# A 3x3 convolution taken by row pairs: four products of row sums and tap sums in place of six

## The chip, the core and the metric

The kernel runs on one core of a Trainium2 chip. The metric is device time in microseconds (us), from the start to the end of one execution. The kernel before takes 14228.68 us (median of 3 runs, 14222.29 to 14232.47).

The engines of the core work beside each other, each through its own instructions in order: PE (matrix products into PSUM), DVE and POOL (elementwise work on SBUF; DVE also reads PSUM), ACT (functions of one input, with a table of functions that has to be loaded), SP (starts transfers). They wait for each other through semaphores.

## The reference, cut to what matters

Four layers run over 16 images of 192 channels and 32 x 32 pixels. Only layer 0 is touched. Of layer 0 the change touches one operation, the last:

```
seq = group_norm(x) as tokens                       # 1024 tokens of 192 channels
y   = seq + vil_block(seq)                          # layer norm, up-projection to 384, causal
                                                    # convolution over 4 tokens, q, k, v, gates,
                                                    # mLSTM over 12 heads, down-projection
y   = y + silu(seq @ w_lin + b_lin)
out = conv2d(y, conv2_w, 3 x 3, padding 1) + conv2_b    # 192 -> 192 channels
batch_norm(out)                                     # statistics over all 16 images
```

All data is float32. The batch norm needs the convolution of all images, so layers 1 to 3 start when the last image's convolution is done.

## The kernel before, in words

`layer0` handles one image at a time. Image 0 stands alone; a loop (L751) runs images 1 to 15; in iteration b the convolution of image b-1 is worked in between the steps of image b; the convolution of image 15 stands alone behind the loop (L755). The loop ends each iteration with a barrier of all engines.

**An image** (`image`, L403) has three stages.
- The head: group norm (L88 to L107, with two tiny products L91 and L99), channel norm (products with `on192` and, on the squares `sq`, again; L122, L124, L128, L129, L131), the up-projection `w_up` (24 products of 512 columns, all at L39), the causal convolution on DVE (L435, L439), the gates (L455, L466, scans L480, L484), the projections `w_q` and `w_k` (L39), and `qs` (products L549, DVE L553).
- The chunk phase, written out by hand under `tc.manual_schedule()`: twelve times `scores` (products L613 into four PSUM tiles, ACT L620, DVE L624, POOL L627 with `mask`), with `turned` (L584, L594), `leave` (L683, L686, POOL L687) and `finish` (L639, L646, L658, ACT L650, DVE L651, product L671, ACT L672 and L673, DVE L674) as soon as a chunk of 128 tokens has what it needs.
- The tail: `w_lin` and `w_down` (products L731), ACT L735 (Silu), DVE L736, and DVE L739, which writes the sum into the padded image `ypad`.

Outside the chunk phase a scheduler orders the instructions of each engine; inside it, the order is as written, and the scheduler may put tail products between.

**The convolution** (`conv3`, L365) is a generator. `fill(n)` (L563) takes n steps from it. `ypad` holds channels 0 to 127 in one half (e = 0) and channels 128 to 191 in the other, there twice on 64 partitions each, one copy moved by one column by two transfers (`both`, L744), so that two of the three columns go in one product. The result comes in three groups (m): channels 0 to 127 for the upper and the lower 16 rows, and channels 128 to 191 for both halves, side by side on PSUM's partitions. Each group is 15 steps; a step is one product of 512 columns, or two side by side for the third group. So an image takes 45 steps. A group adds up in the one PSUM tile `pc`; then ACT writes it out (L394), DVE takes statistics (L395), SP stores it (L397). The steps are spread: `fill(15)` ahead of the chunk phase (L567), which the scheduler spreads over the head; `fill(2)` in each `finish` (L669) and in each of the rounds without one (L704); 1 (L705) and 8 (L708) at the end.

PSUM tiles for all other products rotate over six (`ps`, L164); the four for `scores` are among them. Layers 1 to 3 (`LayersB`) are planned by another part of the kernel, which the change does not touch.

Of the kernel before, what the change touches and what calls it, by code (L numbers as in the profile page):

```python
# [11 lines left out]
F32 = mybir.dt.float32  # L12
BF16 = mybir.dt.bfloat16
AF = mybir.ActivationFunctionType
ALU = mybir.AluOpType
# [16 lines left out]
def half(hf):  # L32
    return slice(hf * HL, (hf + 1) * HL)
# [113 lines left out]
def rows(ap):  # L147

    return ap.rearrange("p (h w) -> p h w", w=W)
# [3 lines left out]
def layer0(tc, cx, NB, ydram, sdram, w1d):  # L153
    nc, I = cx.nc, cx.I
    with ExitStack() as ctx:
        wp = ctx.enter_context(tc.tile_pool(name="a_w", bufs=1))
# [3 lines left out]
        psc = ctx.enter_context(tc.tile_pool(name="a_psc", bufs=1, space=PSUM))  # L160
# [24 lines left out]
        prp = pre.enter_context(tc.tile_pool(name="a_pre", bufs=1))  # L185
# [14 lines left out]

        hmask = wp.tile([128, 4 * HW1], F32, name="hmask")
        nc.sync.dma_start(hmask, I["c_hmask"])
        b_if = []
        for nm, eng in (("b_i", nc.sync), ("b_f", nc.scalar)):
            t = wp.tile([128, 1], F32, name="v_" + nm)
# [9 lines left out]
        nc.scalar.dma_start(conv_k, I["conv_k"].rearrange("(k p) t -> p k t", p=128))  # L217
        mask = wp.tile([128, 2 * CH], F32, name="mask")

        blocks = wp.tile([128, 4, DH], F32, name="blocks")  # L220
        nc.vector.tensor_copy(blocks, hmask.rearrange("p (j d) -> p j d", d=HW1)[:, :, 0:DH])
        blk = blocks.rearrange("p j d -> p (j d)")

# [78 lines left out]
        p = ps()  # L302
# [30 lines left out]
        w_c2 = wp.tile([128, 9, C], F32, name="w_c2")  # L333
        nc.sync.dma_start(w_c2, I["conv2_wT"][0:128])
        w_c2p = wp.tile([128, 2, 3, C], F32, name="w_c2p")
        for u in range(2):
            r = slice(64 * u, 64 * u + 64)
            taps = I["conv2_wT"][128:C].rearrange("p (y x) o -> p y x o", x=3)
            nc.sync.dma_start(w_c2p[r, 0], taps[:, :, u, :])
            nc.sync.dma_start(w_c2p[r, 1], taps[:, :, 2, :])  # L340
# [8 lines left out]
        b_down, b_lin, c2_b = vec3("b_down"), vec3("b_lin"), vec3("conv2_b")  # L349
        x_in = wp.tile([128, 3, L + 3], F32, name="x_in")  # L350
        nc.gpsimd.memset(x_in, 0.0)
        ypad = wp.tile([128, 2, H + 2, W + 2], F32, name="ypad")
        nc.gpsimd.memset(ypad, 0.0)
        vas = []
        for i in range(2):
            t = wp.tile([128, NH, DH], F32, name="va%d" % i)
# [7 lines left out]

        def conv3(b):  # L365

            st = sm.tile([128, 3, 6], F32, tag="st", name="st")
# [3 lines left out]
            def window(r, e, y, x, hf):  # L371
                return ypad[r, e, 16 * hf + y : 16 * hf + y + 16, x : x + W]

            for m in range(3):
                p = psc.tile([128, HL], F32, name="pc")

                parts = [(m, slice(0, 128), slice(0, 128))] if m < 2 else [
                    (0, slice(128, C), lower), (1, slice(128, C), upper)
                ]
                for n in range(15):  # L380
                    for hf, o, r in parts:
                        y, x = divmod(n, 3) if n < 9 else ((n - 9) % 3, 2 * (n >= 12))
                        if n < 9:
                            w_, v = w_c2[:, n, o], window(slice(0, 128), 0, y, x, hf)
                        elif n < 12:
                            w_, v = w_c2p[:, 0, y, o], window(slice(0, 128), 1, y, x, hf)
                        elif hf == 0:
                            w_, v = w_c2p[lower, 1, y, o], window(lower, 1, y, x, hf)
                        else:
                            w_, v = w_c2p[upper, 1, y, o], window(upper, 1, y, x - 1, hf)  # L390
                        nc.tensor.matmul(p[r, :], lhsT=w_, rhs=v, start=(n == 0), stop=(n == 14))  # L391
                    yield
                yo = wk2.tile([128, HL], F32, tag="yo", name="yo", bufs=1)
                nc.scalar.activation(yo, p, AF.Identity, bias=c2_b[:, m // 2 : m // 2 + 1])  # L394
                nc.vector.bn_stats(st[:, m, :], yo)  # L395
                for hf, o, r in parts:
                    nc.sync.dma_start(here(o)[:, half(hf)], yo[r, :])  # L397
            stats = lambda o: sdram[bass.ds(b, 1), o].rearrange("o p s -> p (o s)")
            nc.scalar.dma_start(stats(slice(0, 128)), st[:, 0:2, :].rearrange("p h s -> p (h s)"))
            for hf, r in enumerate((lower, upper)):  # L400
                nc.scalar.dma_start(stats(slice(128, C))[:, 6 * hf : 6 * hf + 6], st[r, 2, :])

        def image(b, conv):  # L403
            xn = big.tile([P6, 2, L], F32, name="xn")
# [6 lines left out]
            sq = big.tile([P6, 2, L], F32, tag="kT", name="sq")  # L411
# [32 lines left out]


            cx.ln_exp()
            it = gp.tile([128, L], F32, name="it")
            lf = gp.tile([128, L], F32, name="lf")
            e1 = gp.tile([128, L], F32, name="e1")

            p = ps()
            for g in range(3):
                for q in range(4):
# [7 lines left out]
            raw = gp.tile([128, HL], F32, name="raw")  # L461
            nc.scalar.copy(raw, p)
            for j in range(2):
                for hf in range(2):
# [13 lines left out]
            for c in range(NCH):  # L478
# [4 lines left out]
            at = gp.tile([128, L], F32, name="at")  # L483
# [20 lines left out]
            kT = big.tile([128, 3, L], F32, tag="kT", name="kT")  # L504
# [19 lines left out]
            nc.vector.tensor_copy(dec.rearrange("p g c -> p (g c)"), p[:, 0 : 3 * NCH])  # L524


            itg = big.tile([128, 3, L], F32, name="itg")
# [35 lines left out]
            def fill(n):  # L563
                for _ in range(n):
                    next(conv, None)

            fill(15)  # L567


            cst = big.tile([128, 3, DH], F32, name="cst")  # L570
# [119 lines left out]
            with tc.manual_schedule():  # L690
                ready = begun = 0
                for n in range(3 * NCH // 2):
                    scores(n)
                    if begun < NCH and 2 * n + 1 >= 3 * begun:
                        turned(begun)
                        begun += 1
                    if normed:
                        leave()

                    if 2 * n >= 3 * ready + 3:  # L700
                        finish(ready)
                        ready += 1
                    else:
                        fill(2)  # L704
                fill(1)  # L705
                leave()
                finish(ready)
                fill(8)  # L708
                leave()
# [12 lines left out]
            for n in range(3):  # L722
                e = n // 2
                parts = [(n, slice(0, 128), slice(0, 128))] if n < 2 else [
                    (0, slice(128, C), lower), (1, slice(128, C), upper)
                ]
                pl, pd = ps(), ps()
                for p, w_, v, k in ((pl, w_lin, xn, 2), (pd, w_down, hT, 3)):
                    for i in range(k):
                        for hf, o, r in parts:  # L730
                            nc.tensor.matmul(  # L731
                                p[r, :], lhsT=w_[:, i, o], rhs=v[:, i, half(hf)], start=(i == 0), stop=(i == k - 1)
                            )
                lin = wk2.tile([128, HL], F32, tag="lin", name="lin")
                nc.scalar.activation(lin, pl, AF.Silu, bias=b_lin[:, e : e + 1])  # L735
                nc.vector.tensor_add(lin, lin, xr[:, n, :])  # L736
                for hf, o, r in parts:
                    x = 0 if r == upper else 1
                    nc.vector.scalar_tensor_tensor(  # L739
                        ypad[r, e, 1 + 16 * hf : 17 + 16 * hf, x : x + W], rows(pd[r, :]),  # L740
                        b_down[r, e : e + 1], rows(lin[r, :]), op0=ALU.add, op1=ALU.add,
                    )

        def both():  # L744

            lower, upper = slice(0, 64), slice(64, 128)
            nc.sync.dma_start(ypad[upper, 1, 1:17, 0:W], ypad[lower, 1, 1:17, 1 : 1 + W])
            nc.sync.dma_start(ypad[lower, 1, 17:33, 1 : 1 + W], ypad[upper, 1, 17:33, 0:W])

        image(0, iter(()))  # L750
        with tc.For_i(1, NB, 1) as b:  # L751
# [107 lines left out]
class LayersB:  # L859
# [1314 lines left out]
```

## Time and profile before

| what | value |
|---|---|
| median of the runs | 14228.68 us |
| the profiled execution | 14239.71 us |
| its span, first to last instruction | 14237.9 us |
| image 0 and what is ahead of it | 0 to 206.7 us |
| loop, 15 iterations | 206.7 to 3049.5 us |
| spacing of iterations | by turns 188.1 and 190.9 us, save the first: mean 189.5 |
| last convolution alone | 3049.8 to 3094.4 us |
| layers 1 to 3 | the rest, about 11140 us |

How to read the views: the page lists each engine's busy time and, in 40 slices of the span (356 us each), its share in tenths. The window view gives, for a stretch, each engine's busy time and instruction count, and the clock that PE was granted as a share of full speed. The timeline lists instructions in order with start, duration, engine, line, tile written and read, how many were merged, and in brackets the idle time ahead and what ended it. A float32 product shows as two records; with 512 columns two records take 0.86 us.

### The profile page before, as it was taken

What the parts mean: (1) busy time and instruction counts of PE and PEld (TensorE: products, weight loads), DVE (VectorE), ACT (ScalarE), POOL (GpSimd) and SP (SyncE); (2) the same over time, 40 slices, a digit from 0 to 9 for tenths busy, and PEclk for the clock granted to TensorE, in tenths of its full rate; (3) what the DMA queues carried; (4) which work ended last, traced back from release to release, by engine and by line L of the source; (5) the groups of instructions that cost most, each with busy time, mean ns of one, the idle gap of its engine ahead of it and who ended that gap; (6) DMA issues with size and microseconds to landing.
All of it is one profiled execution on the core that took longest, in us unless ns stands there. A gap on an engine that the chain in (4) does not pass through costs nothing. (4 is left out here: it accounts for less than half of the span.)

```text
span 14237.9 us, 185312 instructions
## 1 busy us (share of the span) xinstructions
PE 12109.3 (85%) x68762; PEld 4953.3 (35%) x68762; DVE 11818.6 (83%) x9084; ACT 8686.4 (61%) x12225; POOL 10919.5 (77%) x6319
## 2 busy tenths in 40 slices
PE   8999999987888888888888888888888888888877
PEld 4444444442232333333333333333333333333323
DVE  4444444446899999999999999999999999999996
ACT  3333333335666676767676767667676767676665
POOL 2222222215789999999999999999999999999995
PEclk9999999998999999999999999999999999999988
DMA  1000000013344544444444445454544444444432
GB/s 29 15 16 15 16 16 14 14 39 125 129 161 136 164 142 159 153 166 158 146 160 145 161 142 164 153 165 141 166 137 165 141 162 163 156 155 151 147 123 90
DMA packets 702526, 1707.93 MB, mean 120 GB/s; under 512 B 125456, under 2 KB 260064, under 8 KB 693984
## 3 DMA queue, kind: packets, MB, share of 16 engines
q1 hardware_dynamic: 688928, 1693.28, 36.0%
q8 instruction: 555, 9.09, 0.3%
q10 hardware_dynamic: 12736, 3.04, 0.1%
q14 instruction: 307, 2.51, 0.1%
HBM read 1338.12 MB, written 341.15 MB: 118 GB/s over the span
## 5 line engine op out<-in xcount | busy, mean ns | idle before, releaser
L1995 POOL TENSOR_TENSOR xs<-du,bb 128x1024 f32<-128x1024 f32 x3072 | 7191.9, 2365 | 313.2 <-DVE h L2003 309.0
L2003 DVE TENSOR_TENSOR_SCAN h<-h,xs 128x1024 f32<-128x1024 f32 x2688 | 6149.3, 2288 | 280.9 <-ACT h L1988 191.4
L1988 ACT ACTIVATE h<-dl,A 128x1024 f32<-128x1024 f32 x3072 | 3415.4, 1113 | 2517.6 <-DVE hc L2012 2358.9
L2012 DVE TENSOR_TENSOR hc<-h,cb 128x1024 f32<-128x1024 f32 x2688 | 3290.2, 1224 | 267.4 <-DVE h L2003 7.3
L2045 PE MATMUL acc<-hc,sel 128*32 128x256 f32 x24576 | 2046.3, 419 | 916.0 <-DVE hc L2012 691.3
L815 PE MATMUL mm<-pad,dg 128*128 128x512 f32 (+1 forms) x5580 | 2672.0, 616 | 97.2 <-ACT pad L815 37.5
L627 POOL TENSOR_TENSOR D<-D,mask 128x256 f32<-128x256 f32 x768 | 543.4, 740 | 2102.2 <-DVE D L624 2102.2
L2045 PEld LDWEIGHTS acc<-hc,sel 128*32 128x32 f32 x24576 | 546.3, 113 | 2899.6 <-DVE hc L2012 1583.4
L815 PEld LDWEIGHTS mm<-pad,dg 128*128 128x128 f32 (+1 forms) x5580 | 958.0, 182 | 1476.4 <-issue 1293.1
L2008 POOL TENSOR_TENSOR hc<-hc,cb 128x1024 f32<-128x1024 f32 x384 | 905.3, 2357 | 149.8 <-DVE hc L2003 145.7
L815 PE MATMUL mm<-pa,wgt 128*128 128x512 f32 (+1 forms) x1408 | 795.9, 691 | 111.2 <-ACT p L815 52.4
L2003 DVE TENSOR_TENSOR_SCAN hc<-h,xs 128x1024 f32<-128x1024 f32 x384 | 875.5, 2280 | 13.7 <-ACT h L1988 9.4
L2053 PE MATMUL acc<-one,zero 128*128 128x512 f32 x1498 | 804.4, 667 | 0.0
L815 POOL TENSOR_TENSOR dlh<-dlh,e 128x512 f32<-128x512 f32 x384 | 490.6, 1278 | 233.8 <-ACT e L815 233.7
L815 POOL TENSOR_TENSOR c<-cx 96x768 f32<-96x768 f32 (+4 forms) x510 | 650.4, 1299 | 0.6 <-ACT cx L815 0.6
L815 PE MATMUL mm<-c,xT 128*96 128x256 f32 x2048 | 570.1, 420 | 64.5 <-ACT c L815 64.4
L815 POOL TENSOR_TENSOR duh<-dlh,xx 128x512 f32<-128x512 f32 x384 | 538.1, 1401 | 30.1
L391 PE MATMUL pc<-ypad,w_c 128*64 128x512 f32 (+1 forms) x1152 | 480.4, 664 | 74.2 <-PEq L751 41.5
L2032 PE MATMUL acc<-y,ident 128*128 128x512 f32 x576 | 350.6, 694 | 185.3 <-ACT y L2064 185.2
L624 DVE SCALAR_TENSOR_TENSOR D<-D,s 128x256 f32<-128x256 f32 x768 | 271.6, 415 | 255.4 <-ACT D L620 255.3
L2064 ACT COPY y<-acc 128x512 f32<-128x512 f32 x384 | 410.8, 1070 | 115.2 <-PE acc L2045 114.4
L815 PE MATMUL mm<-xd,dtw 108*128 108x512 f32 x768 | 455.7, 677 | 15.5 <-ACT p L815 13.7
(333 smaller groups left out, 15741.3 us busy)
## 6 DMA issues: line engine op xcount, KB each, us to landing
dl<-dld SPq DMA_DIRECT2D x768, 512.0 KB
du<-dud SPq DMA_DIRECT2D x768, 512.0 KB
bb<-xdr SPq DMA_DIRECT2D x256, 512.0 KB
cb<-xdr SPq DMA_DIRECT2D x256, 512.0 KB
dld<-dlh SPq DMA_DIRECT2D x384, 256.0 KB
dud<-duh SPq DMA_DIRECT2D x384, 256.0 KB
dg<-dqd SPq DMA_DIRECT2D x270, 192.0 KB
dg<-dvd SPq DMA_DIRECT2D x180, 144.0 KB
```

What stands on the lines that cost most here:

```text
L391: nc.tensor.matmul(p[r, :], lhsT=w_, rhs=v, start=(n == 0), stop=(n == 14))
L627: nc.gpsimd.tensor_mul(d, d, mask)
L815: return f(out, *args, **kw)
L1988: self.nc.scalar.activation(self.h[u % 2], self.dl[n % 2], AF.Exp, scale=self.A[:, blk, n : n + 1])
L1995: self.nc.gpsimd.tensor_mul(self.xs[u % 3], self.du[n % 2], self.bb[blk])
L2003: self.nc.vector.tensor_tensor_scan(o, h, x, 0.0, op0=ALU.mult, op1=ALU.add)
L2008: self.nc.gpsimd.tensor_mul(h, h, self.cb[u % BLOCKS])
L2012: self.nc.vector.tensor_mul(self.hc[u % 3], self.h[u % 2], self.cb[u % BLOCKS])
L2032: nc.tensor.matmul(acc, lhsT=self.cx.ident, rhs=self.y[:, g, half(pair)], start=True, stop=False)
L2045: nc.tensor.matmul(self.acc[rows4(q), q4(s)], lhsT=self.sel, rhs=part(q), start=False, stop=(s + blk == BLOCKS),)
L2053: self.nc.tensor.matmul(self.acc, lhsT=cx.zero.to_broadcast([128, 128]), rhs=cx.one.to_broadcast([128, HL]), start=False, stop=False,)
L2064: self.nc.scalar.copy(y.rearrange("p (s w h) -> p s h w" if k % 2 == 0 else "p (s h w) -> p s w h", s=2, **turn), self.acc.rearrange("p (s ...
```

## The change

The nine taps form three rows. For output rows 2j and 2j+1 the input rows 2j to 2j+3 are combined once into four sums (`four`): r0-r2, r1+r2, r2-r1, r1-r3; the weights once into four as well: g0, (g0+g1+g2)/2, (g0-g1+g2)/2, g2. Four products p0 to p3 then give the two output rows as p1+p2+p0 and p1-p2-p3. Products p1 and p2 use r1+r2 and r2-r1, p0 and p3 the other two. Each product is over 16 row pairs x 32 columns = 512 columns and takes five steps (three columns of channels 0 to 127, two of the rest). So channels 0 to 127 need 4 x 5 steps, and channels 128 to 191 2 x 5 double steps: 30 in place of 45. There are six groups in place of three, all in the one tile `pc`; p1 is written out by ACT (`one`), the others are added by DVE.

The sums are made by eight POOL operations in `both`, at the head of each iteration. `ypad` shares its memory with `kT` and is cleared by POOL once per image. The weights come in 15 transfers in place of 5, and ten DVE operations make the combined ones, once. To make room, some tiles share others' memory (`yo` with `it`, `one` with `fc`, `lin` with `lf` and `e1`, `sq` with `itg`, `raw` with `at`).

```diff
+        for y, i in ((0, 0), (1, 2), (2, 3)):
+            nc.sync.dma_start(w_c2[:, i], I["conv2_wT"][0:128, 3 * y : 3 * y + 3])
+            for u in range(2):
+                r = slice(64 * u, 64 * u + 64)
+                nc.sync.dma_start(w_c2p[r, i, 0], I["conv2_wT"][128:C, 3 * y + u])
+                nc.sync.dma_start(w_c2p[r, i, 1], I["conv2_wT"][128:C, 3 * y + 2])
+        for w in (w_c2, w_c2p):
+            w = w.rearrange("p i x o -> p i (x o)")
+            nc.vector.tensor_add(w[:, 1], w[:, 0], w[:, 3])
+            nc.vector.tensor_add(w[:, 1], w[:, 1], w[:, 2])
+            nc.vector.scalar_tensor_tensor(w[:, 2], w[:, 2], -2.0, w[:, 1], op0=ALU.mult, op1=ALU.add)
+            nc.vector.tensor_scalar(w[:, 1], w[:, 1], 0.5, None, op0=ALU.mult)
+            nc.vector.tensor_scalar(w[:, 2], w[:, 2], 0.5, None, op0=ALU.mult)
...
-        ypad = wp.tile([128, 2, H + 2, W + 2], F32, name="ypad")
-        nc.gpsimd.memset(ypad, 0.0)
+        kT = wp.tile([128, 3, L], F32, name="kT")
+        pad = kT.rearrange("p g t -> p (g t)")[:, 0 : 2 * (H + 2) * (W + 2)]
+        four = wp.tile([128, 2, 4, H // 2, W + 2], F32, name="four")
...
+            for e, o in enumerate((slice(0, 128), slice(128, C))):
+                yo = gp.tile([128, L], F32, tag="it", name="yo")[0:np_]
+                one = big.tile([128, L], F32, tag="fc", name="one")[0:np_, 0:HL]
+                for group in ((1,), (2,), (0,), (3,)) if e == 0 else ((1, 2), (0, 3)):
+                    p = psc.tile([128, HL], F32, name="pc")
+                    parts = [(i, p) for i in group] if e == 0 else [(group[0], p[lower]), (group[1], p[upper])]
+                    for n in range(5):
+                        for k, (i, q) in enumerate(parts):
+                            term(q, i, n, o, upper if k else lower)
+                        yield
+                    for i, q in parts:
+                        if i == 1:
+                            nc.scalar.activation(one, q, AF.Identity, bias=c2_b[0:np_, e : e + 1])
+                        elif i == 2:
+                            nc.vector.tensor_add(even, rows(one), rows(q))
+                            nc.vector.tensor_sub(odd, rows(one), rows(q))
+                        elif i == 0:
+                            nc.vector.tensor_add(even, even, rows(q))
+                        else:
+                            nc.vector.tensor_sub(odd, odd, rows(q))
+                    yield
+                for hf in range(2):
+                    nc.vector.bn_stats(st[0:np_, 2 * e + hf, :], yo[:, half(hf)])
+                nc.sync.dma_start(here(o), yo)
...
-            fill(15)
+            fill(12)
...
                     else:
-                        fill(2)
+                        fill(1)
+                nc.gpsimd.memset(pad, 0.0)
                 fill(1)
                 leave()
...
         def both():
...
+            for e in range(2):
+                r = [ypad[:, e, k : k + H - 1 : 2, :] for k in range(4)]
+                nc.gpsimd.tensor_sub(four[:, e, 0], r[0], r[2])
+                nc.gpsimd.tensor_add(four[:, e, 1], r[1], r[2])
+                nc.gpsimd.tensor_sub(four[:, e, 2], r[2], r[1])
+                nc.gpsimd.tensor_sub(four[:, e, 3], r[1], r[3])
```

A group now takes six calls of the generator: five steps and one that only writes out.

More of the change, by code (lines that the diff above doesn't have):

```diff
@@ L199, in layer0 @@
         mh_b = vec("mh_b", 128, nc.scalar)
-        hmask = wp.tile([128, 4 * HW1], F32, name="hmask")
+        hmask = prp.tile([128, 4 * HW1], F32, name="hmask")
         nc.sync.dma_start(hmask, I["c_hmask"])
@@ L218, in layer0 @@
         mask = wp.tile([128, 2 * CH], F32, name="mask")
-        blocks = wp.tile([128, 4, DH], F32, name="blocks")
+        blocks = prp.tile([128, 4, DH], F32, name="blocks")
         nc.vector.tensor_copy(blocks, hmask.rearrange("p (j d) -> p j d", d=HW1)[:, :, 0:DH])
@@ L332, in layer0 @@
             nc.sync.dma_start(t, I[nm].rearrange("(k p) o -> p k o", p=p))
[L333 to L340, printed above, removed]
+        w_c2 = wp.tile([128, 4, 3, C], F32, name="w_c2")
+        w_c2p = wp.tile([128, 4, 2, C], F32, name="w_c2p")
+        for y, i in ((0, 0), (1, 2), (2, 3)):
[11 more added lines that the diff above has]
+            nc.vector.tensor_scalar(w[:, 2], w[:, 2], 0.5, None, op0=ALU.mult)
         def vec3(name):
@@ L351, in layer0 @@
         nc.gpsimd.memset(x_in, 0.0)
-        ypad = wp.tile([128, 2, H + 2, W + 2], F32, name="ypad")
-        nc.gpsimd.memset(ypad, 0.0)
+        kT = wp.tile([128, 3, L], F32, name="kT")
+        pad = kT.rearrange("p g t -> p (g t)")[:, 0 : 2 * (H + 2) * (W + 2)]
+        ypad = pad.rearrange("p (e y x) -> p e y x", e=2, x=W + 2)
+        four = wp.tile([128, 2, 4, H // 2, W + 2], F32, name="four")
         vas = []
@@ L365, in conv3 @@
         def conv3(b):
-            st = sm.tile([128, 3, 6], F32, tag="st", name="st")
+            st = sm.tile([128, 4, 6], F32, tag="st", name="st")
             here = lambda o: ydram[bass.ds(b, 1), o].rearrange("o p l -> p (o l)")
             lower, upper = slice(0, 64), slice(64, 128)
[L371 to L388, printed above, removed]
-                        else:
-                            w_, v = w_c2p[upper, 1, y, o], window(upper, 1, y, x - 1, hf)
-                        nc.tensor.matmul(p[r, :], lhsT=w_, rhs=v, start=(n == 0), stop=(n == 14))
@@ new lines, in term @@
+            def term(out, i, n, o, r):
+                if n < 3:
+                    w_, v = w_c2[:, i, n, o], four[:, 0, i, :, n : n + W]
+                elif n == 3:
+                    w_, v = w_c2p[:, i, 0, o], four[:, 1, i, :, 0:W]
+                else:
+                    x = 2 if r == lower else 1
+                    w_, v = w_c2p[r, i, 1, o], four[r, 1, i, :, x : x + W]
+                nc.tensor.matmul(out, lhsT=w_, rhs=v, start=(n == 0), stop=(n == 4))
+            for e, o in enumerate((slice(0, 128), slice(128, C))):
+                np_ = o.stop - o.start
+                yo = gp.tile([128, L], F32, tag="it", name="yo")[0:np_]
+                even, odd = (yo.rearrange("p (j u w) -> p j u w", u=2, w=W)[:, :, u, :] for u in range(2))
+                one = big.tile([128, L], F32, tag="fc", name="one")[0:np_, 0:HL]
[14 more added lines that the diff above has]
+                            nc.vector.tensor_add(even, even, rows(q))
+                        else:
+                            nc.vector.tensor_sub(odd, odd, rows(q))
@@ L392, in conv3 @@
                     yield
[L393 to L397, printed above, removed]
+                for hf in range(2):
+                    nc.vector.bn_stats(st[0:np_, 2 * e + hf, :], yo[:, half(hf)])
+                nc.sync.dma_start(here(o), yo)
@@ L398, in conv3 @@
             stats = lambda o: sdram[bass.ds(b, 1), o].rearrange("o p s -> p (o s)")
             nc.scalar.dma_start(stats(slice(0, 128)), st[:, 0:2, :].rearrange("p h s -> p (h s)"))
-            for hf, r in enumerate((lower, upper)):
-                nc.scalar.dma_start(stats(slice(128, C))[:, 6 * hf : 6 * hf + 6], st[r, 2, :])
+            nc.scalar.dma_start(stats(slice(128, C)), st[lower, 2:4, :].rearrange("p h s -> p (h s)"))
         def image(b, conv):
@@ L410, in image @@
             h = big.tile([P6, 2, L], F32, tag="h", name="h")
-            sq = big.tile([P6, 2, L], F32, tag="kT", name="sq")
+            sq = big.tile([P6, 2, L], F32, tag="itg", name="sq")
             rstd = big.tile([P6, L], F32, tag="fc", name="rstd")
@@ L446, in image @@
             cx.ln_exp()
-            it = gp.tile([128, L], F32, name="it")
-            lf = gp.tile([128, L], F32, name="lf")
-            e1 = gp.tile([128, L], F32, name="e1")
+            it = gp.tile([128, L], F32, tag="it", name="it")
+            lf = gp.tile([128, L], F32, tag="lf", name="lf")
+            e1 = gp.tile([128, L], F32, tag="e1", name="e1")
             p = ps()
@@ L460, in image @@
                     )
-            raw = gp.tile([128, HL], F32, name="raw")
+            raw = gp.tile([128, L], F32, tag="at", name="raw")[:, 0:HL]
             nc.scalar.copy(raw, p)
@@ L482, in image @@
                 )
-            at = gp.tile([128, L], F32, name="at")
+            at = gp.tile([128, L], F32, tag="at", name="at")
             nc.vector.tensor_tensor_scan(at, lf, it, 0.0, op0=ALU.add, op1=ALU.max)
@@ L503, in image @@
             qT = big.tile([128, 3, L], F32, name="qT")
-            kT = big.tile([128, 3, L], F32, tag="kT", name="kT")
             for m in range(3):
@@ L524, in image @@
             nc.vector.tensor_copy(dec.rearrange("p g c -> p (g c)"), p[:, 0 : 3 * NCH])
-            itg = big.tile([128, 3, L], F32, name="itg")
+            itg = big.tile([128, 3, L], F32, tag="itg", name="itg")
             for g in range(3):
@@ L733, in image @@
                             )
-                lin = wk2.tile([128, HL], F32, tag="lin", name="lin")
+                lin = gp.tile([128, L], F32, tag="lf" if n == 1 else "e1", name="lin")[:, 0:HL]
                 nc.scalar.activation(lin, pl, AF.Silu, bias=b_lin[:, e : e + 1])
```

## The prediction

> **What bounds the kernel now.** I read the page's slices first, then the window view by stage, then the timeline of one iteration (968.0 to 1156.1 us). From the page:
>
> ```profile
> span 14237.9 us, 185312 instructions
> ...
> PE   8999999987888888888888888888888888888877
> ...
> DVE  4444444446899999999999999999999999999996
> ...
> POOL 2222222215789999999999999999999999999995
> ```
>
> Layer 0 is the first nine slices: PE has nine tenths, DVE four, POOL two. Later DVE and POOL are full, and nothing is changed there. So only PE's path through layer 0 counts. From the window view (PE, PEld, DVE, ACT, POOL, then PEclk):
>
> ```profile
> 968.00:976.00 8.00, 7.91 (x18) 3.56 (x19) 5.07 (x14) 2.82 (x3) 0.00 (x0) 0.81 0.23 38
> 1054.50:1064.00 9.50, 8.23 (x73) 4.98 (x77) 2.64 (x6) 2.75 (x7) 3.58 (x5) 0.64 0.08 29
> 1064.00:1140.00 76.00, 72.85 (x1070) 43.61 (x1062) 33.56 (x81) 30.78 (x82) 42.02 (x57) 1.00 0.05 16
> 57.00:81.00 24.00, 23.97 (x52) 10.28 (x56) 18.18 (x19) 5.92 (x9) 0.00 (x0) 0.87 0.00 0
> 124.00:195.00 71.00, 58.19 (x1043) 42.17 (x1035) 37.14 (x89) 39.38 (x94) 45.78 (x62) 1.00 0.05 13
> ```
>
> The last two rows are image 0, which has no convolution beside it: its chunk phase takes 71 us, that of the loop some 84. So 30 steps of 0.86 us (26 us of PE) lengthen that phase by 13 us; the other half hides in PE's waits. The clock column is the second finding: PE runs at 0.64 in the 9.5 us behind one wait. The timeline of PE shows which:
>
> ```profile
> 1050.20 1.99 PE L549 MATMUL ps<-isc,sel 32*128 32x512 f32 x12
> 1054.49 1.21 PE L613 MATMUL s<-at,itg 32*128 32x128 f32 x13 [2.30 <-DVE qs L553]
> ...
> 1057.46 0.85 PE L594 MATMUL ps<-ident,kT 128*128 128x128 f32 x3
> 1059.46 3.78 PE L391 MATMUL pc<-ypad,w_c 128*128 128x512 f32 x4 [1.16 <-ACT yo L394]
> 1063.17 0.73 PE L613 MATMUL s<-at,itg 32*128 32x128 f32 x16
> ```
>
> An idle time of 2.30 us, then four records take 3.78 us; at full clock they take 1.88 (next round). Steps of the convolution are work and also what keeps PE's clock up.
>
> **The change, part by part**, against that iteration.
>
> *Removed.* 15 of 45 steps: 12.9 us of PE per image. The order of the changed kernel's instructions shows where: the head keeps 5 of 15 steps, all ahead of the channel norm; 5 more stand between L549 and the first L613; the chunk phase and the tail hold 20 in place of 30.
>
> *Start of the iteration: slower, +2.6 us.* PE's first product now waits for the second POOL sum, its fourth for the sixth; L91, L99 and the channel norm stand behind them in PE's queue. The price of a sum over 544 elements is not in the trace. Nearest rows: POOL L627 over 256 takes 740 ns, `dlh` over 512 takes 1278, so 2.1 ns for each further element and 1.35 us; the strided L687 (915 for 384) and `duh` (1401 for 512) bound it at 1.2 to 1.5. So the first product goes at 970.8 and not at 968.1; at half clock step, L91, step, L99 end at 975.2; the third step follows, the sixth sum is there at 976.2, two more steps end at 978.3. There the channel norm's products start, which started at 975.7. Ends: +1.5 (clock up early) and +5.0 (DVE's small operations of the group norm each wait for a POOL operation). For the latter the rows disagree: DVE L667 takes 243 ns alone and up to 782 beside POOL, but L2012, also two inputs from SBUF, 1202 to 1227 beside a full POOL. I go with L2012, which has 2688 instances.
>
> The Trainium skill (SBUF — State Buffer, "Who interferes with whom") says that a DVE instruction with two SBUF inputs and a POOL instruction that reads SBUF shut each other out for a whole instruction. By it L95, L96 and L97 would wait some 3.4 us (an estimate), and the sum below would come to about +16 us instead; L667 agrees, L2012 does not.
>
> *Head without filler: +3.8 us.* The channel norm's second products (on `sq`) and the up-projection follow idle times that steps filled. Without these I get 2.4 us ahead of `sq` (975.7 plus 8 records end at 979.2, `sq` is ready at 981.6) and 3.3 us ahead of `w_up` (L128 0.68, L129 1.06, L131 1.2 and hand-overs). By the 2.30 us above both lower the clock. Image 0 shows the price: from the first `w_up` product to DVE's L435, 7.5 us (57.03 to 64.57) against 4.6 (989.32 to 993.92); from the first `sq` product to the second L128 5.4 against 4.1. I take +2.7 and +1.4, less 0.3 for the steps that stood ahead of `w_up`. From L435 on DVE sets the pace to the gates (16.1 us in both images). Ends: -0.3 (clock holds) and +5.6 (all eight `sq` records at half clock, 3.0 later, and 2.9). Between L455 and L466 one step goes: -0.2.
>
> The skill's TensorE: Matmul & The Clock Gate ("Why this matters for your kernels") puts the limit at gaps over about 3 us. By it the gap ahead of `sq` would be free, and the sum 21 us lower; the trace's 2.30 us with a clock of 0.64 behind it speaks against.
>
> *Start of the chunk phase: -3.2 us.* The five steps now fill the 2.30 us and PE stays at full clock: they end at 1056.5, the first L613 goes there (1054.5 before). DVE's L624 stands behind the two new additions of p2, which need the group's end: 1058.6 in place of 1056.5. The second round's L613 then goes at 1060.0 instead of 1063.2, since the wait for L394 (1.16) and the half clock are gone. POOL's masks come next: two rounds of 2.8 with a `vw` of 0.84 between, from 1059.1, let the first `finish` go on at 1065.6; with its two steps L671 starts at 1067.9, before at 1071.1. Ends -1 (masks back up further) and -5.
>
> *Rest of the chunk phase: -5.0 us.* Rounds without `finish`: from L683 to the next L613 0.87 us in image 0 (144.97 to 145.83), 2.6 with two steps (1082.85 to 1085.44), 3.8 where L394 is waited for (1102.22 to 1106.00). With one step, none and one: -0.9, -2.9, -0.9. In `finish` two steps cost only 0.4 (L658 to L671: 1.7 in image 0, 2.1 in the loop), since L651 is awaited anyway; one fewer there: -0.3. DVE's additions (0.7 each) and statistics (1.4) stand where DVE waits 1.9 us for L673. Ends -3 and -6.
>
> *Tail: +0.3 us.* The scheduler moves the first Silu and five `w_lin`/`w_down` products into the last rounds. The Silu costs table loads (1.28 each) ahead of L672 and L673, as in image 0; two of them are on the path. One step also waits for ACT and DVE to write p1 and p2 out. I get the last L683 3.9 us later, and behind it four DVE operations (2.8 us) ahead of L686; but 8.5 products are left where 14 were (-4.7). Ends -1.5 and +3.
>
> *Hidden.* The clearing by POOL (2.02 us, L353) stands ahead of two L687, in a gap from 1129.7 to 1133.8; without that, +2.0 per image. At the start ten transfers (0.65 each on SP) and ten DVE operations (5.2 us) fall in DVE's 7.8 us wait ahead of L131 in image 0; without that up to +5 once. The last convolution, alone: 30 steps, but six write-outs and the POOL sums ahead; 43.5 us against 44.7: -1, from -3 to +4.
>
> **Sum.** 2.6 + 3.8 - 0.2 - 3.2 - 5.0 + 0.3 = -1.7 us. Every second iteration takes 190.9 us rather than 188.1, with a clock of 0.61 in its first 8 us and 0.58 behind the 2.30 us wait; half of that should go: -0.6 on the mean. So -2.3 x 15 - 1 = -35.5 us: 14239.7 becomes 14204.2 on the profiled execution's scale, which is 11.0 above the median; on the median's 14193.
>
> **Rivals.**
> - *The head goes cold.* Place: from the iteration's start to `w_up`. PE starts late and in pieces, so the clock stays at half through the five steps (they end at 980.3, so +4.6), both norms and the first `w_up` products: `sq` +3.0, `w_up` +2.9, -0.3, sum +10.2; the other terms as above, -8.1: +2.1 for the iteration. It decides from a loss of 8.7 us in the head on (the 8.1 of the other terms and the 0.6 of every second iteration). 15 x 2.1 - 1 for the last convolution: +31, 14260. For it: the 0.81 and 0.61 with PE's start as it is. Against: image 0's `sq` phase got its clock back.
> - *The clock holds in the head.* Only the wait for POOL is left: 2.6 - 0.3 in place of 6.4, -6.4 per iteration, 14132. For it: between 976 and 990 the clock is 1.00. Against: that is with filler.
> - *What goes was free.* POOL's masks and the DVE additions hold the chunk phase, gaining 5 rather than 8.2 and losing what the head loses: within 15 us of zero, 14225.
> - *Fewer products in name only*: excluded; the changed order has 40 matmuls per image where 60 were.
>
> **Chances.** Forecast .39 (.28 faster, .11 within 0.2%), clock holds .17 (faster), free .12 (same), cold head .32 (.29 slower, .03 same). Together faster .45, same .26, slower .29; 0.2% (28 us) is about what a measurement of this kernel tells from no change. The ends of the terms alone reach from about -11.5 to +9.4 per iteration; all at one end at once is unlikely, so the range goes from 14120, past the second rival, to 14285, past the first; outside it some .08 below and .1 above.
>
> **What would show it.** Right: L613's first round at full clock, spacing of iterations near 187; PE idle behind POOL for some 2.7 us at the iteration's start; window clocks under 0.9 at `sq` and `w_up`; two table loads more around L672 and L673. Wrong: POOL sums over 1.5 us, DVE's L95 to L97 above 0.16 us, a first L613 with an idle time ahead, or L687 waiting for the clearing.

## The result, and the profile after

The changed kernel takes 14273.2 us, median of 10 runs (14249.84 to 14302.78); the kernel before took 14227.38 us in its 10 runs (14219.52 to 14248.12). The ratio is 1.0032, 95% interval 1.0022 to 1.0041: slower by a third of a per cent. The forecast was 14193, faster; the time lies inside its range, on the side of its first rival.

The page of the changed kernel, its span and the slices of PE, DVE and POOL:

```profile
span 14282.5 us, 184150 instructions
...
PE   8999999987888888888888888888888888888877
...
DVE  5555455546899999999999999999999999999996
...
POOL 2223332224789999999999999999999999999995
```

The span is 44.6 us longer. The slices hardly show it: DVE and POOL have a tenth more in layer 0, PE the same nine tenths, although it does a third fewer convolution steps. So PE's time there went into waiting and into products at half clock, as the views below show. Split by the ends of the stages, image 0 is 5.4 us shorter (200.5 us in place of 205.9 to PE's last tail product), the fifteen iterations are 56.7 longer together, the last convolution 1.9 shorter, layers 1 to 3 4.8 shorter.

Within an iteration I took the first start of each product in PE's timeline, and the mean over iterations 1 to 14 (in us; "head" runs from the end of the last w_down product to the first product on xn, "norm" from there to the first w_up product, "up" to the first product of the gates, "gates" to the first product L549 for qs, "rest" to the end of the tail; "spacing" is the time from the end of one tail to the next):

| run | head | norm | up | gates | rest | spacing | ratio to before (95%) |
|---|---|---|---|---|---|---|---|
| before | 11.8 | 13.2 | 20.8 | 40.1 | 103.7 | 189.55 | 1 |
| changed | 16.5 | 16.7 | 24.0 | 39.8 | 96.2 | 193.13 | 1.0032 (1.0022-1.0041) |
| lock | 13.2 | 13.2 | 20.8 | 40.1 | 101.1 | 188.29 | 0.9983 (0.9974-0.9992) |
| delay | 13.1 | 12.7 | 20.8 | 39.8 | 101.3 | 187.81 | 0.9975 (0.9965-0.9985) |
| third | 9.5 | 14.9 | 23.9 | 39.8 | 97.9 | 185.98 | 0.9965 (0.9951-0.9979) |
| nosum | 9.6 | 13.3 | 23.7 | 39.8 | 96.1 | 182.63 | 0.9923 (0.9910-0.9936) |
| nolock | 12.7 | 13.4 | 23.7 | 39.8 | 96.2 | 185.84 | 0.9960 (0.9946-0.9974) |
| tail0 | 14.0 | 17.1 | 23.9 | 39.8 | 96.2 | 190.95 | 1.0020 (1.0011-1.0029) |
| one12 | 14.6 | 13.5 | 21.5 | 39.8 | 96.1 | 185.49 | 0.9972 (0.9963-0.9981) |
| adelay | 18.1 | 16.8 | 23.7 | 39.8 | 96.1 | 194.48 | 1.0056 (1.0042-1.0070) |
| split | 11.5 | 13.7 | 22.8 | 39.8 | 96.1 | 183.98 | 0.9930 (0.9917-0.9943) |
| so18 | 10.6 | 13.3 | 20.9 | 40.1 | 96.6 | 181.40 | 0.9908 (0.9893-0.9923) |
| so18b | 9.7 | 15.4 | 20.9 | 40.1 | 96.3 | 182.43 | 0.9942 (0.9929-0.9956) |
| so18c | 9.1 | 14.8 | 20.9 | 40.1 | 96.5 | 181.38 | 0.9920 (0.9906-0.9933) |

Each row is of one profiled execution, which lies up to 19 us from the median of its runs (one12: 14165.97 against 14185.24), or 1.3 us in a spacing. The second row against the first is the story of the change: 7.5 us gained in the rest, 11.3 lost in head, norm and up. The window view of the changed kernel (PE, PEld, DVE, ACT, POOL, then PEclk) for the iteration that starts at 978.7 us:

```profile
978.70:986.70 8.00, 4.16 (x6) 1.49 (x6) 5.83 (x11) 1.24 (x1) 7.97 (x7) 0.53 0.22 35
986.70:1000.20 13.50, 12.88 (x16) 4.08 (x16) 3.51 (x7) 1.54 (x2) 1.80 (x2) 0.52 0.22 58
1002.00:1016.00 14.00, 10.88 (x15) 4.12 (x16) 2.36 (x3) 4.58 (x5) 0.00 (x0) 0.66 0.00 0
1080.80:1090.30 9.50, 9.28 (x168) 6.91 (x168) 5.54 (x15) 5.62 (x17) 7.37 (x11) 1.00 0.01 2
1090.30:1160.60 70.30, 66.25 (x949) 38.94 (x947) 35.00 (x81) 34.81 (x78) 40.08 (x53) 1.00 0.07 21
```

Rows four and five are the chunk phase, at full clock from its first product (it was 0.64 there); from its first scores to the start of the last L699 (L683 before) it takes 79.8 us on the mean, 86.3 before. Rows one to three are the head: half clock for 21.5 us on end, 17.0 of them with PE busy, then 0.66 into the up-projection. The timeline of the same iteration, PE with DVE and POOL, shows how that comes about:

```profile
980.04 1.15 POOL L769 TENSOR_TENSOR four<-kT 128x544 f32<-128x544 f32 x1
...
981.24 2.08 PE L388 MATMUL pc<-four,w_c 128*128 128x512 f32 x2 [5.44 <-POOL four L769]
...
983.61 1.35 POOL L768 TENSOR_TENSOR four<-kT 128x544 f32<-128x544 f32 x1
983.71 1.26 DVE L95 TENSOR_TENSOR gn_d<-gn_mv,gn_mg 96x2 f32<-96x2 f32 x1
984.92 1.15 POOL L769 TENSOR_TENSOR four<-kT 128x544 f32<-128x544 f32 x1
985.00 1.08 DVE L96 TENSOR_TENSOR gn_d<-gn_d 96x2 f32<-96x2 f32 x1
986.03 1.15 POOL L770 TENSOR_TENSOR four<-kT 128x544 f32<-128x544 f32 x1
986.12 1.07 DVE L97 TENSOR_TENSOR gn_d<-gn_d,gn_mv 96x2 f32<-96x2 f32 x1
...
987.25 0.48 PE L99 MATMUL ps<-gn_d,blk 96*96 96x2 f32 x2 [1.85 <-DVE gn_d L97]
...
993.28 6.84 PE L39 MATMUL ps<-xn,on 96*96 96x512 f32 x8
...
1010.47 2.93 PE L39 MATMUL ps<-h,w_up 96*128 96x512 f32 x3 [3.12 <-DVE h L131]
```

The same places in an iteration of the kernel before:

```profile
968.09 3.44 PE L391 MATMUL pc<-ypad,w_c 128*128 128x512 f32 x4 [2.96 <-PEq L751]
...
971.85 0.16 DVE L95 TENSOR_TENSOR gn_d<-gn_mv,gn_mg 96x2 f32<-96x2 f32 x1
...
976.15 3.60 PE L39 MATMUL ps<-xn,on 96*96 96x512 f32 x8
```

PE's first product waits for the second sum, as forecast (5.44 us of idle time where it was 2.96). But look at DVE: L95, L96 and L97 work on two elements, and each ends within 0.02 us of the end of a POOL sum. They took 0.16 us each before. So L99 stands 1.85 us late, the steps behind it start late, and the channel norm's eight products take 6.84 us in place of 3.60.

### The profile page after: what moved, and what is told of

The parts are those of the page before. It is cut to its first block, busy times and chain, and to the rows that moved or that the text cites. A ratio compares the mean times of both kernels' runs of the same rounds, so it can differ in the third digit from the quotient of the medians.

```text
span 14282.5 us, 184150 instructions
## 1 busy us (share of the span) xinstructions
PE 12026.4 (84%) x68122; PEld 4874.3 (34%) x68122; DVE 11961.1 (84%) x9238; ACT 8768.1 (61%) x12284; POOL 11104.8 (78%) x6462
## 5 line engine op out<-in xcount | busy, mean ns | idle before, releaser
L2026 DVE TENSOR_TENSOR_SCAN hc<-h,xs 128x1024 f32<-128x1024 f32 x384 | 875.6, 2280 | 14.3 <-ACT h L2011 10.5
L838 PEld LDWEIGHTS mm<-c,xT 128*96 128x96 f32 x2048 | 338.9, 176 | 316.1 <-issue 104.4
L838 PEld LDWEIGHTS mm<-pa,wgt 128*128 128x128 f32 (+1 forms) x1408 | 260.8, 206 | 490.0 <-issue 232.0
```

The lines of the kernel that those rows point to most:

```text
L838: return f(out, *args, **kw)
L2026: self.nc.vector.tensor_tensor_scan(o, h, x, 0.0, op0=ALU.mult, op1=ALU.add)
```

## The experiments

Three causes were on the table for the lost 11.3 us: DVE held by POOL's sums and PE's clock with it (A, later C), the missing steps in the head alone (B), and PE's late start alone (D).

### lock: the sums beside the old kernel

```diff
+            for e in range(2):
+                r = [ypad[:, e, k : k + H - 1 : 2, :] for k in range(4)]
+                for i, j in ((0, 2), (1, 2), (2, 1), (1, 3)):
+                    nc.gpsimd.tensor_sub(spare, r[i], r[j])
```

> The kernel before, with the changed kernel's eight POOL operations at the head of each iteration (each over 544 elements of the padded image, into a spare tile that nobody reads). Theory A (the sums and the missing steps together keep PE's clock down: the sums hold DVE's L95 to L97, so L99 comes late): L95 to L97 take about 1.1 us each in place of 0.16, L99 comes some 2 us later, an iteration is 1 to 4 us longer, so 14240 to 14290 us. Rival B (only the missing steps matter, POOL beside DVE costs nothing): L95 to L97 stay at 0.16, 14225 to 14235.

Measured: 14213.14 against 14237.97 us. DVE's timeline of an iteration:

```profile
966.90 1.00 DVE L95 TENSOR_TENSOR gn_d<-gn_mv,gn_mg 96x2 f32<-96x2 f32 x1
967.94 0.16 DVE L96 TENSOR_TENSOR gn_d<-gn_d 96x2 f32<-96x2 f32 x1
968.13 1.20 DVE L97 TENSOR_TENSOR gn_d<-gn_d,gn_mv 96x2 f32<-96x2 f32 x1
...
970.24 2.41 DVE L107 TENSOR_SCALAR xn<-xnext,gn_mg,gn_rs 96x1024 f32<-96x1024 f32 x2
```

The holding up is real without anything else of the change: L95 1.00 at the median where it was 0.16, L107 2.41 for what takes 1.53, L99 1.3 us later on the mean. Yet the kernel became faster, which neither theory allowed. The gain is all in the rest: the first scores still follow an idle time of 2.30 us, but the window behind it, 0.64 before, is now

```profile
1051.40:1060.90 9.50, 8.11 (x89) 5.62 (x90) 4.09 (x10) 4.50 (x13) 4.81 (x7) 1.00 0.08 29
```

The same wait, and no loss of clock; the run delay, below, takes that up.

### third: fewer steps without sums

```diff
-                for n in range(15):
+                for n in (0, 1, 2, 9, 12, 3, 4, 5, 10, 13):
...
-            fill(15)
+            fill(5)
...
-                        fill(2)
+                        fill(1)
```

> The kernel before, with the products of the third tap row left out (30 steps in place of 45, and so another output), five of them in the head, ahead of the channel norm, as in the changed kernel; no sums, no other write-outs. A: the clock comes up in the first 5 us as before; what is lost is some 4 us in the gaps ahead of sq and w_up; the chunk phase gains 7 to 9: 3 to 6 us less per iteration, 14135 to 14185. B (the missing steps alone make the head 11 us longer): 3 us more per iteration, 14260 to 14285.

Measured: spacing 185.98, 14173.7 us, as A had it. With PE starting at once, five steps in the head cost 3.1 us in "up" and 1.7 in "norm", and the head itself got 2.4 shorter. The missing steps alone do not make the loss: the rest gains 5.8. (Two of the nine runs took 14231.84 and 14246.71 us, the other seven 14162.85 to 14176.47; why, no run here tells.)

### nosum: the change without its sums

```diff
-            for e in range(2):
-                r = [ypad[:, e, k : k + H - 1 : 2, :] for k in range(4)]
-                nc.gpsimd.tensor_sub(four[:, e, 0], r[0], r[2])
...
+        for e in range(2):
+            for i in range(4):
+                nc.gpsimd.tensor_copy(four[:, e, i], ypad[:, e, i : i + H - 1 : 2, :])
```

> The changed kernel without the sums inside the loop (they are replaced by eight copies, made once ahead of the loop, and the output is another). A: PE starts some 2.3 us earlier, L95 to L97 take 0.16 and L99 comes 2 us earlier, the clock is up before the channel norm ends, and an iteration takes 184 to 188: 14120 to 14190. B: only the wait of 2.3 us goes, 14235 to 14245.

Measured: spacing 182.63, 10.5 us less than the changed kernel, 14128.19 us. B falls: the sums, 10 us of POOL time that nothing in the profile's totals shows as scarce, cost as much on the path of PE.

### nolock and tail0: DVE held, or PE late?

```diff
-    nc.vector.tensor_sub(d, mv[:, :, 0], mg)
-    nc.vector.tensor_mul(d, d, d)
-    nc.vector.tensor_add(d, d, mv[:, :, 1])
+    nc.vector.tensor_sub(d, mv[:, :, 0], p[0:P6, 0:2])
+    for a in range(2):
+        nc.vector.tensor_scalar(
+            d[:, a : a + 1], d[:, a : a + 1], d[:, a : a + 1], mv[:, a, 1:2], op0=ALU.mult, op1=ALU.add
+        )
```

> The changed kernel with the group norm's three small additions and products written so that DVE reads one tensor from SBUF in each (the mean straight from PSUM, then two operations with the others as scalars of the partition): the sums stay on POOL at the head of the iteration, and PE's first step still waits for them. C (it is DVE's waits behind POOL's sums, and the gap that they make ahead of L99, that keep PE's clock down): L99 2 to 3 us earlier, the clock up before the channel norm ends, spacing 184 to 188, 14130 to 14200. D (it is PE's late start): only the 2 to 3 us go, spacing 190 to 191.5, 14215 to 14245.

Measured: spacing 185.84, 14182.57 us. The sums are as before on POOL, PE waits 5.44 us for them, and still 7.3 of the 10.5 us are back. From the timeline of nolock (here L101 is the product that was L99):

```profile
763.15 2.07 PE L390 MATMUL pc<-four,w_c 128*128 128x512 f32 x2 [5.44 <-POOL four L771]
...
765.50 0.14 DVE L95 TENSOR_TENSOR gn_d<-gn_mv,ps 96x2 f32<-96x2 f32 x1
765.56 1.35 POOL L770 TENSOR_TENSOR four<-kT 128x544 f32<-128x544 f32 x1
765.68 0.45 DVE L97 TENSOR_SCALAR gn_d<-gn_d,gn_mv 96x1 f32<-96x1 f32 x2
...
767.10 0.37 PE L101 MATMUL ps<-gn_d,blk 96*96 96x2 f32 x2
...
770.41 3.90 PE L39 MATMUL ps<-xn,on 96*96 96x512 f32 x8
```

With one tensor from SBUF per operation these small operations pass by POOL's sum, L101 follows without an idle time, and the eight products on xn take 3.90 us, nearly all at full clock. That is C. One tensor from SBUF is no way out for every operation: the group norm's last (L107, here L109) has only one, and takes 3.44 us for a pair in this iteration, 1.53 in the changed kernel.

tail0 takes PE's wait away instead (sums of channels 0 to 127 at the end of the image, the others at the head, on POOL). Against the run split, below:

```diff
-            if one:
-                sums(1, nc.vector, True)
...
+            sums(1, nc.gpsimd)
```

> The changed kernel with the sums of channels 0 to 127 at the end of the image (as in the run split), and those of channels 128 to 191 still on POOL at the head of the iteration, where they meet the group norm. C: L95 to L97 are late, the clock stays down, spacing 190 to 194, 14230 to 14275. D: PE starts without waiting, spacing 184 to 188, 14130 to 14190.

Measured: spacing 190.95, 14266.11 us: C's time, but not by C's way. L95 to L97 are at 0.16, since POOL has to wait for the two transfers; the sums then meet L107, and two steps that stand ahead of the channel norm wait for them:

```profile
1164.91 5.78 POOL L377 TENSOR_TENSOR four<-kT 128x544 f32<-128x544 f32 x4 [6.11 <-DMA kT<-kT]
...
1166.56 2.91 DVE L107 TENSOR_SCALAR xn<-xnext,gn_mg,gn_rs 96x1024 f32<-96x1024 f32 x2
1167.42 2.31 PE L395 MATMUL pc<-four,w_c2p 128*128 128x512 f32 x4 [1.38 <-POOL four L377]
...
1169.66 6.89 PE L39 MATMUL ps<-xn,on 96*96 96x512 f32 x8
```

A gap of 1.38 us in PE's stream ahead of the channel norm, and the products on xn are at half clock again, 6.89 us. So D falls, PE's early start alone gains 2.2 us; and C has to be put more widely: what can cost is a gap that the sums tear into PE's stream between its first product and the channel norm, whichever operation they hold. Not every such gap does (so18, below).

### one12: the missing steps again, with the sums

```diff
-                one = big.tile([128, L], F32, tag="fc", name="one")[0:np_, 0:HL]
+                one = big.tile([128, HL], F32, name="one")[0:np_]
...
-                    d = wk2.tile([128, 2 * CH], F32, tag="D", name="D", bufs=14)
+                    d = wk2.tile([128, 2 * CH], F32, tag="D", name="D", bufs=12)
```

> The changed kernel with memory of its own for the tile one and two fewer buffers for D: ten steps in the head in place of five (three ahead of sq, two ahead of w_up), the sums as in the changed kernel. C (the sums at the head are the main cost, the missing steps a smaller one): L95 to L97 and L99 as late as before, the channel norm still at half clock, w_up to the gates back near 20.8: spacing 187 to 191, 14190 to 14240. Rival B (the missing steps alone are the cause): spacing 181 to 184, 14100 to 14140.

Measured: spacing 185.49, 14185.24 us; "up" back to 21.5. Better than C had it, less than B: the second group of five steps, which could not start in the head because `one` shared memory with `fc`, wins 7.6 us, and nolock 7.3. By the medians, each against the kernel before in the same measurement, it is 5.7 and 7.0 us an iteration. L96 and L97 still take 1.07 us in one12, and L99 is as late as in the changed kernel, to within 0.4 us: what the waiting costs depends on how many steps stand beside it. 11.3 us were lost in all, so the two causes hardly add; I read it so that they meet in PE's clock, and either remedy brings part of it up.

### delay and adelay: the clock's raster

```diff
+    for _ in range(7):
+        nc.vector.tensor_scalar(d, d, 1.0, None, op0=ALU.mult)
```

The same two lines behind L97, in the kernel before (delay) and in the changed one (adelay).

> The kernel before with seven more small operations (times 1.0) on DVE behind L97, which make L99 some 1.3 us later; POOL does nothing new. Theory R (an iteration settles on whole periods of the clock's raster, 3.413 us: 111 in two iterations before, 55 in one with the eight idle POOL operations, so what helped in the run lock was the shift): spacing 187.7 in most iterations, 14205 to 14225, faster than before. Rival (POOL's work itself helped, a delay costs its length): spacing 190.5 to 191, 14240 to 14260.

> The changed kernel with the seven small operations of the run delay behind L97. R (iterations settle on the clock's raster): the spacing stays at 57 periods, 194.56, in most iterations or goes to 58, 197.97; 14265 to 14320, no 1.3 us per iteration. Rival (a delay costs its length): 195.9 in an iteration that took 194.6, 14285 to 14300 with no spacing at a whole number of periods.

Measured: delay 14206.78 against 14242.35 us, faster, with spacings of 187.51 and 187.96 by turns. Seven useless operations that put L99 1.8 us further behind L91 make an iteration 1.7 us shorter. So a shift alone is enough for what lock gained; that POOL's work had no part in it is not shown. adelay: L99 is 2.8 us later on the mean, and the spacing is 194.5 to 194.7 in twelve of fourteen iterations, where the changed kernel had 194.6 to 194.8 in nine; the mean rises only from 193.13 to 194.48, and 14306.32 us (1.0056) goes with the short iterations being lost.

The spacings of these runs fit one period of 3.4133 us, the number of periods being mine to choose: before 188.04 + 190.84 = 111 periods, changed 194.57 = 57, lock 187.72 = 55, delay 187.51 + 187.96 = 110, nosum 181.46 + 183.77 = 107, tail0 191.14 = 56, third 182.42 + 186.33 + 187.61 = 163, each to within 0.03 us. The traces have that period without any choice: in all 14 the granted clock is 0.5 or 1.0 and nothing else, and it changes only on a raster (a fixed grid in time) of 3.4133 us, to within 0.003 us over the whole execution. That an iteration shifts against the raster until it repeats itself fits this and is not shown.

The raster also tells what a gap costs. I divided each trace along its own raster, up to 3100 us, and took the share of each window that PE was busy. The 2.30 us wait ahead of the first scores falls into two windows in both kernels; first the kernel before, from the second of them on, then lock, from the first on:

```profile
1052.98:1056.40 3.42, 1.79 (x34) 1.48 (x34) 2.05 (x4) 0.29 (x2) 0.00 (x0) 1.00 0.00 0
1056.40:1059.81 3.41, 2.25 (x10) 1.85 (x10) 1.78 (x5) 2.46 (x7) 2.72 (x4) 0.50 0.02 5
```

```profile
1047.23:1050.65 3.42, 1.90 (x12) 0.61 (x12) 2.56 (x5) 0.50 (x1) 0.00 (x0) 1.00 0.00 0
1050.65:1054.06 3.41, 2.52 (x40) 2.21 (x41) 1.92 (x5) 1.02 (x4) 0.10 (x1) 1.00 0.02 5
```

A window busy for 0.52 of its time was followed by half clock, one busy for 0.56 was not. Over all 14 traces, windows at full clock go like this: busy under 0.40, all 372 were followed by half clock; busy 0.65 and more, 5 of 10507; between, 200 of 460, so there the busy share alone does not decide. Out of half clock, none of 331 windows busy under 0.80 was followed by full clock, but 578 of 716 that were busy 0.90 and more. So half clock costs at least one well filled window, and the 1.85 us gap ahead of L99 in the changed kernel falls into two windows at half clock (from 982.63 and 986.04), which it leaves busy 0.81 and 0.65; behind neither did the clock come up.

The Trainium skill (TensorE: Matmul & The Clock Gate, "What's actually happening") says that the clock is judged in a free-running window of 3413 ns; the runs agree. The same page's rule ("Why this matters for your kernels") that only gaps over about 3 us cost the clock does not hold here: 1.38 in tail0 did (its window was busy 0.60) and so did 2.30 in the kernel before, while 2.30 in lock did not; what is left busy of the window counts.

### split, so18, so18b, so18c: a version that keeps the gain

split makes the sums of channels 0 to 127 on POOL at the end of the image, and the others on DVE behind L107:

```diff
+        def sums(e, eng, pin=False):
...
+            if one:
+                sums(1, nc.vector, True)
...
+            sums(0, nc.gpsimd)
```

> The changed kernel with the sums of channels 0 to 127 made by POOL at the end of the image that writes them, and those of channels 128 to 191 by DVE behind the group norm's last operation; so PE has three steps without waiting, and POOL and DVE don't meet. A: spacing 186 to 190, 14150 to 14215, with sq still or half cold where the two DVE-fed steps come late. B: the missing steps still cost 11 us in the head, 14230 to 14260.

Measured: spacing 183.98, 14139.88 us, a little better than A had it. A sum of 544 elements takes 0.66 us on DVE (four in a row 2.62), 1.15 to 1.36 on POOL in the iteration shown above.

so18 adds the memory for `one` and a third group ahead of the scores:

```diff
+                one = big.tile([128, HL], F32, name="one")[0:np_]
...
-            fill(12)
+            fill(18)
...
+                    d = wk2.tile([128, 2 * CH], F32, tag="D", name="D", bufs=12)
```

> The run split with memory of its own for the tile one (which shared that of the gates' fc, so that the second group could not start in the head), two fewer buffers for D to make room, and fill(18) in place of fill(12): ten steps in the head, four of them ahead of w_up, five ahead of the first scores. A: PE stays at full clock from sq on, w_up to the gates 20.8 us in place of 22.8, five steps fewer in the chunk phase; spacing 177 to 181, 14040 to 14095. Rival (the two buffers of D were needed, or the clock's raster takes the gain): spacing 183 to 185, 14130 to 14150.

Measured: 14106.5 us against 14242.35 of before in the same call, ratio 0.9908 (0.9893 to 0.9923); spacing 181.40, just above the forecast. It is 0.9% faster than the kernel before, and has the lowest time of all; the interval of so18c, below, overlaps its own. The window view of so18, from the iteration's start to w_up, and the first 14 us of w_up:

```profile
1298.50:1306.50 8.00, 6.50 (x14) 2.91 (x15) 6.15 (x16) 2.75 (x3) 0.00 (x0) 0.79 0.23 38
1306.50:1317.80 11.30, 10.80 (x25) 4.04 (x24) 5.24 (x9) 6.28 (x7) 0.00 (x0) 1.00 0.23 67
1317.80:1332.00 14.20, 14.20 (x34) 6.20 (x34) 11.87 (x14) 1.86 (x3) 0.00 (x0) 1.00 0.00 0
```

Full clock from the channel norm on, where the changed kernel has 0.52 and 0.66.

so18b leaves two sums at the end of the image, so that the loop's barrier comes earlier, and puts six on POOL behind L107; so18c mends that only the first of the six waited:

```diff
+                sums(*rest, behind=normal)
...
+            sums((0, 1), (0, 2))
```

> The run so18 with only two sums (r1+r2 and r2-r1 of channels 0 to 127) at the end of the image, so that the loop's barrier comes 1.4 us earlier, and the other six on POOL, made to wait for the group norm's last operation on DVE, so that DVE is not held by them before the channel norm. Every piece counts: 2 to 3 us less per iteration, spacing 178.4 to 179.5, 14055 to 14085. Rival (the raster takes the gain): spacing 181.0 to 181.4, 14095 to 14110.

Measured: spacing 182.43, 14140.51 us, above both forecasts. Five of the sums ran ahead and met L107, the old fault once more:

```profile
941.04 3.54 DVE L107 TENSOR_SCALAR xn<-xnext,gn_mg,gn_rs 96x1024 f32<-96x1024 f32 x2
```

> The run so18b with all six later sums made to wait for the group norm's last operation (there only the first of them was, the others ran ahead and held that operation for 3.5 us in place of 1.5). Every piece counts: L107 at 1.5 us, xn in one piece, sq 6.1 us behind xn; 2 to 3 us less per iteration than so18: spacing 178.4 to 179.5, 14060 to 14085. Rival (the clock's raster takes it): 181.0 to 181.5, 14095 to 14115.

Measured: spacing 181.38, 14112.64 us, no better than so18. Head 9.1 in place of 10.6, norm 14.8 in place of 13.3: in one iteration of each, PE waits 1.48 us ahead of xn in both kernels, and the eight products behind it take 6.71 us in so18c and 3.65 in so18. The clock took what the earlier start gave, as the rival said, though here the spacings are no whole numbers of periods. The 1.48 us left a window busy 0.57 in so18, and full clock followed; in so18c one busy 0.52, and half clock followed.

## Why the prediction was wrong

**The forecast was off by 80 us of span, and in its sign**: -35.5 foretold, +44.6 measured; the loop alone -34.5 against +56.7.

- *Rest of the iteration, right.* The start of the chunk phase, its rest and the tail were to give 7.9 us, and gave 7.5. In the iteration from 781 us the first L671 (L687 in the changed kernel) comes 17.45 us behind the first L549 (L565), 20.90 before (22.26 in every other iteration): 3.45 sooner (foretold 3.2), in a first round at full clock; L455 to L466 gave 0.24 (0.2).
- *Up, nearly right.* The loss behind a `w_up` without filler was put at 2.7, and is 3.2.
- *Start of the iteration, wrong.* +2.6 was taken, +4.7 measured. The price of a sum was right (1.35 was taken; 1.15 and 1.36 measured), and so was PE's first wait (2.7; 2.5, from 2.96 to 5.44). One reading was off: the products on xn started at 976.15 in the kernel before, not at 975.7, so by its own working the term was +2.1, and the gap ahead of `sq` 1.9 and not 2.4 (1.86 measured). The step that failed was the choice between two rows for DVE's small operations beside POOL: "I go with L2012", that is, no cost. L95 to L97 take 3.4 us in the iteration shown, 0.5 before, which the prediction had named as a sign of being wrong. With that waiting taken away (nolock) an iteration is 3.7 us shorter than before, where the forecast had 2.3. L2012 has 1024 elements and shows no such waiting; why not, no run here tells. An operation of two elements does show it: it takes 0.16 us alone, so the rest of its time is POOL's.
- *Norm, wrong.* No loss on the products on xn was foretold and 1.7 us measured; 1.1 on `sq`, and 1.8 measured. In the iteration shown both go with the failed step: behind the gap ahead of L99 twelve records that were counted at full speed ran at half clock (four took 3.92 us, eight 6.84). The step alone does not fix their price: with ten steps in the head in place of five (one12) and L99 as late, "norm" is back at 13.5. The first rival had the clock at half through the five steps, both norms and the first `w_up` products; its 10.2 us for the head are close to the 11.3 measured, its cause (PE's late start) is not what nolock and tail0 show.
- *The rule set aside holds for L95 to L97.* The Trainium skill (SBUF — State Buffer, "Who interferes with whom") says that a DVE instruction with two SBUF inputs waits for a POOL instruction that reads SBUF, and the other way round, and that one with at most one such input does not, outside the modes that use two ports. The prediction gave it a price, a sum of +16 us, and did not take it. L95 went from 0.16 to 1.26 us; nolock, which takes the second input away, brings it to 0.14. L2012, at 1202 to 1227 ns beside a full POOL, still speaks against a wait behind every POOL operation.
- *Parity, wrong.* -0.6 was taken for the slower of two alternating iterations. The alternation goes with the 111 periods in two iterations; the changed kernel has no such turns, and its spacings are 188.2 to 194.8. A small shift need not come out with its own sign there: in delay, L99 1.8 us later gave an iteration 1.7 us shorter.
- *Image 0* is 5.4 us shorter, not foretold. L107 waited 5.41 us there and waits 0.47 now. Its start varies between the runs with POOL and the loads at the setup; the cause is open. The 4.8 us in layers 1 to 3 are less than the runs of one kernel differ (14219.52 to 14248.12 us before).

What stays open beside these: the exact rule of the clock. Windows busy between 0.40 and 0.65 go either way, and in the changed kernel PE was busy for 12.9 us at half clock, three full windows on end among them, before the clock came up.

## What to carry to other kernels

Work taken off the engine that bounds a stage can be lost again if what is put on another engine stands ahead of it: here a third of the convolution's products paid for eight sums placed where a chain of tiny operations crosses two engines, and the gain appeared once the sums were moved behind that chain. Look for small DVE operations with two tensors in SBUF beside POOL, and price them by POOL's instruction, not by their own. And in a loop, judge a change of a few us by several placements: the clock's raster can hide it (so18c) or turn its sign (delay).

## What the runs showed of the hardware

- DVE and POOL: L95 with two SBUF inputs took 1.26 us at the median of its 16 instances in the changed kernel (0.16 before); L107, of one input and two scalars, took 2.4 to 3.5 us for a pair beside POOL (lock, nolock, tail0, so18b), 1.53 alone.
- A delay can make a loop faster: +1.8 us ahead of L99 gave -1.7 us per iteration.
- The same idle time of PE left the clock at half in one kernel and not in another: 2.30 us (0.64 before, 1.00 in lock), 1.48 us (6.71 and 3.65 us for eight records).
- The clock is 0.5 or 1.0 and changes only every 3.4133 us: a window with PE busy under 0.40 was always followed by half clock (372 of 372), one busy 0.65 and more almost never (5 of 10507).
